# Half 0's output blocks between the steps of half 1's first modes: four blocks ahead, in other tiles

## The chip, the core and the metric

The kernel runs on one core of a Trainium2 chip. The metric is device time in microseconds (us), the median of several runs. The core has five engines that run side by side, each in its own program order: TensorE (PE, matmuls), VectorE (DVE), ScalarE (ACT), GpSimd (POOL) and SyncE (SP), which here only issues DMAs. POOL and ACT issue some DMAs too. All DMAs are carried by 16 DMA engines. SBUF has 128 partitions, and the matmuls write PSUM, in banks of 512 floats for each partition.

## The reference, cut to what matters

The program has two layers over an image of 256 x 256 x 128 floats. Layer 0 is a gated attention. Layer 1, in whose last third the change lies, is a Fourier operator block. Its 256 channels are tokens of 256 x 128 pixels, in groups of four:

```python
h0 = instance_norm(attn, norm2_w, norm2_b)
h1 = fno_layer(h0, mix_wr[0], mix_wi[0], mix_bias[0], mix_sw[0], mix_sb[0], (H, W), norm=True, act=True)
h2 = fno_layer(h1, mix_wr[1], mix_wi[1], mix_bias[1], mix_sw[1], mix_sb[1], (H, W), norm=True)
out = instance_norm(h2, mon_w, mon_b) + attn
...
def fno_layer(x, wr, wi, bias, sw, sb, out_hw, norm=False, act=False):
    skip = jnp.einsum('bihw,oi->bohw', x, sw) + sb[:, None, None]
    xf = spectral_conv(x, wr, wi, bias, out_hw)
    if norm:
        xf = instance_norm(xf)
    y = xf + skip
    return gelu(y) if act else y
```

A spectral convolution takes the few lowest Fourier modes of an image, mixes them over the four channels of a group, and turns them into an image again. The skip is a 4 x 4 mix of the channels pixel by pixel. At the end `x` (the input of the layer) is added.

## The kernel before, in words

The 256 tokens are two halves of 128, one token for each partition. An image is cut into 16 blocks of NB = 2048 pixels (two parts of HB = 1024). A large tile `blocks` holds one half's image, 16 blocks of 1 MB; `hb[b]` is block b. It is used by half 0 first and then by half 1, block after block.

Each half goes through five stages:

- `y_blocks`: the image that enters (half 0's stays in `blocks`, half 1's goes to DRAM, `yd`), with its statistics.
- `first_modes(a)` (L1624): statistics become scales on DVE; the modes are mixed (`mix_modes`: products on DVE or POOL, sums on PE); `norm` takes their energy (`x1ens`, 16 matmuls on PE) and makes rsqrt of it in some ten small steps on DVE and ACT; `synth_modes` (L728) turns the mixed modes, in four steps c0 to c3, into modes for each image row: matmuls (L764 for half 1: `g11gp`), copies by ACT and DVE into a tile `gt`, and four DMAs from the queues of POOL and ACT into DRAM (`Gd1`). Between c1 and c2 the scales of the images (`bl0`, `turn`) are made by small steps on DVE and PE.
- `first_images(a)` (L1695): for each block b, the skip (64 or 32 matmuls, L1387) and the modes' image (32 matmuls, L1372) into four PSUM banks `ups`, the gelu on ACT into `hb[b]`, which overwrites what was there. For block b - 1: transposes (`htps`), copies (`hT`), the skip's statistics (`sps`), and a Fourier step over one axis (`psA`, `yA`), written to DRAM (`Yd`). It yields twice in an iteration, once between these two groups of steps (0) and once at its end (1). Its loads of iteration b fetch block b + 1: half 1's image from `yd` in two parts (tiles of the tags wx and yt) and four DMAs of modes (gs2).
- `second_modes(0)`: the same for the second convolution, from `Yd` to `Gd2`. For half 1 it is `LastModes.run`, after the loop.
- `output(a, b)` (L2072): skip and modes' image into four banks `h2ps`, ACT scales and shifts them into `hb[b]`; a yield; then two DVE adds of `hb[b]` onto `w` (the sum of `x` and a part of the result, made earlier and kept in DRAM, `wd`) and two output DMAs of 512 KB from POOL's queue (L2085, L2086).

The order of all engines, SP's queue among them, is written out by hand in this part (`manual_schedule` with SP), so every instruction stands in its engine's queue in the order in which the Python code makes it. An instruction that waits holds all that stands behind it on its engine. Waits themselves come from the tiles: a tile of a pool and tag is one of a few buffers, and a new user of a buffer waits for the last reader of the old one. A pool that is opened after another was closed takes the same memory.

The main part (L2166 to L2229) runs half 0's stages and those of half 1, woven into each other by generators. The part around the change:

- In pool `mp1` half 0's second modes use the tiles F (4 KB for each partition), gt (8 KB), m (two of 2 KB) and f (4 KB), made in this order. Half 1's first modes `m1` run step by step with them, in tiles of the pool `xp` that stays open (tags yt, gs and xt).
- `output_0` yields after its first load, and then twice for each block: after the matmuls and ACT, and after the adds and the output DMAs. Its loads are `w_b` (1 MB) into the tag xt, of which there are three buffers, and four DMAs of modes into the tag gs.
- L2200 makes `o0`, and its first `next` loads block 0. Then `m1` runs to its end, block 0 of the output follows, and block 1 in the pool `hp1`, which is opened in the place of `mp1`; its tiles are wx (4 KB), gs2 (two of 2 KB), hT (four of 2 KB) and yA (two of 2 KB). Image 0 of half 1 uses loads that were made in `mp1` (`y2` in gt, `g2` in m).
- In the loop over `first_images(1)`, a half-step of the output follows each yield, steered by `due`: blocks 2 to 10 in iterations 0 to 8, and blocks 11 to 15 a little later. The output of block b must be finished before image b of half 1 overwrites `hb[b]`.

Of the kernel before, what the change touches and what calls it, by code (L numbers as in the profile page):

```python
# [10 lines left out]
FP = mybir.dt.float32  # L11
# [7 lines left out]
P = 128  # L19
# [681 lines left out]
def layer1(tc, I, C, ident, x1d, upool, U, Q2, groups, out):  # L701
# [6 lines left out]
    nc = tc.nc  # L708
    NT, H, W = 256, 256, 128
    L = lambda n: I["L1_conv_" + n]  # L710
    with ExitStack() as ctx:
# [86 lines left out]
        wp = gctx.enter_context(tc.tile_pool(name="wp", bufs=3))  # L798
# [363 lines left out]
        NB = 2048  # L1162
        x1v = x1d.rearrange("(a p) h w -> p a (h w)", p=P)
        xp = yctx.enter_context(tc.tile_pool(name="xp", bufs=2))
# [29 lines left out]
        wp = hctx.enter_context(tc.tile_pool(name="wp2", bufs=2))  # L1194
# [86 lines left out]
        with tc.manual_schedule(engines=COMPUTE):  # L1281
# [29 lines left out]
            m1 = sp.tile([32, NT], FP, name="m1")  # L1311
# [41 lines left out]
        ydv = yd.rearrange("(a p) x -> p a x", p=P)  # L1353
        outv = out.rearrange("(a p) h w -> p a (h w)", p=P)
        HB = NB // 2
# [36 lines left out]
        def load_modes(gs, Gd, b, tt=None):  # L1392
            for j in range(4):
                q = slice(32 * j, 32 * j + 32)
                if tt is None:
                    nc.sync.dma_start(
                        gs[q].rearrange("f n t -> f (n t)"),
                        Gd[:, j, 4 * b : 4 * b + 4, :].rearrange("f n t -> f (n t)"),
                    )
                else:  # L1400
                    nc.sync.dma_start(gs[q], Gd[:, j, 4 * b : 4 * b + 4, tt])

        def weave(main, side):

            due = 0.0
            for t in main:
                due += t
                while due > 0 and side is not None:
                    u = next(side, None)
                    if u is None:  # L1410
                        side = None
                        break
                    due -= u

        def run(stage):
            for _ in stage:
                pass
# [50 lines left out]
        halves = []  # L1468
# [10 lines left out]
        wd = dram.tile([P, 16 * NB], FP, name="wd")  # L1479
# [592 lines left out]
        def output(a, b, gs, w, psk):  # L2072

            krs, c0 = (halves[a].col[:, k : k + 1] for k in (14, 9))
            ps = [psk.tile(f"h2ps_{a}_{b}_{j}") for j in range(4)]
            skip(ps, by_turn(hb[b]), by_blocks(halves[a].bl0), False)
            image(ps, gs, bs4)
            for j in range(4):
                nc.scalar.activation(  # L2079
                    by_turn(hb[b])[:, j], rows_of(ps[j]), AF.Identity, bias=c0, scale=krs  # L2080
                )
            yield
            for s in range(2):
                px = slice(b * NB + s * HB, b * NB + (s + 1) * HB)
                nc.vector.tensor_tensor(w[s], w[s], hb[b][:, s * HB : (s + 1) * HB], ALU.add)  # L2085
                nc.gpsimd.dma_start(outv[:, a, px], w[s])  # L2086

        def output_0(psk):

            got = {}  # L2090

            def load(b):
                t = xp.tile([P, NB], FP, tag="xt", name=f"w_{b}", bufs=3)
                nc.sync.dma_start(t, wd[:, b * NB : (b + 1) * NB])
                t = [t[:, 0:HB], t[:, HB:]]
                gs = xp.tile([P, 4, P], FP, tag="gs", name=f"gs3_0_{b}", bufs=3)
                load_modes(gs, halves[0].Gd2, b)
                got[b] = t, gs

            load(0)  # L2100
            yield
            for b in range(16):
                if b not in got:
                    load(b)
                if b < 15:
                    load(b + 1)
                t, gs = got.pop(b)
                yield from output(0, b, gs, t, psk)
                yield
# [56 lines left out]
        with tc.manual_schedule(engines=COMPUTE | {ENG.SP}):  # L2166
            with tc.tile_pool(name="psy", bufs=8, space=PSUM) as psy:
                run(y_blocks(0, Banks(psy, "y"), 0, 32))
            pz = _Held(tc.tile_pool(name="pz", bufs=4, space=PSUM))
            bq, br = Banks(pz.pool, "q"), Banks(pz.pool, "r")  # L2170

            def tiles(wp):
                return Tiles(F=(wp, "F", 1), f=(wp, "f", 1), m=(wp, "m", 2))

            U1 = 24
            with tc.tile_pool(name="mp0", bufs=1) as wp:
                y1 = y_blocks(1, br, 0, U1, Sums(wp))
                weave((2.4 * t for t in first_modes(0, wp, tiles(wp), bq, [(wp, "gt", 1)])), y1)
                halves[0].sums = True
                run(y1)  # L2180
            with tc.tile_pool(name="hp0", bufs=2) as wp:
                run(first_images(0, wp, xp, bq, br))
            with tc.tile_pool(name="mp1", bufs=1) as wp:
                y1 = y_blocks(1, br, U1, 32)
                next(y1)
                m0 = second_modes(
                    0, wp, tiles(wp), bq, [(xp, "xt", 3)], [(wp, "gt", 1)] * 3 + [(xp, "xt", 3)]
                )
                weave((2.4 * next(m0) for _ in range(3)), y1)
                run(y1)  # L2190
                m1 = first_modes(
                    1, wp, Tiles(F=(xp, "yt", 2), f=(xp, "yt", 2), m=(xp, "gs", 3)), br, [(xp, "xt", 3)]
                )
                next(m1)
                for k, _ in enumerate(iter(lambda: next(m0), None)):
                    if k % 4 == 3:
                        next(m1)
                for _ in m0:
                    next(m1, None)
                o0 = output_0(bq)  # L2200
                next(o0)
                y2 = wp.tile([P, NB], FP, tag="gt", name="y2_0", bufs=1)
                nc.sync.dma_start(y2, ydv[:, 1, 0:NB])
                run(m1)
                g2 = wp.tile([P, 4, P], FP, tag="m", name="gs2_1_0", bufs=2)
                next(o0)
                load_modes(g2, halves[1].Gd1, 0)
                next(o0)
            with tc.tile_pool(name="hp1", bufs=2) as hp:
                next(o0)  # L2210
                next(o0)
                due, begun = 0.0, False
                for done in first_images(1, hp, xp, bq, br, ([y2[:, 0:HB], y2[:, HB:]], g2)):
                    if not done:
                        due += 0.9
                        begun = due > 0
                    if begun:
                        next(o0, None)
                    if done and begun:
                        due -= 1.0  # L2220
                run(o0)
            pz.release_now()
            op = ctx.enter_context(tc.tile_pool(name="op1", bufs=1))
            o1, last = Output1(op), LastModes(op)
            last.load()
            with tc.tile_pool(name="mpq3", bufs=1, space=PSUM) as psq:
                last.run(psq, o1)
            with tc.tile_pool(name="opk1", bufs=8, space=PSUM) as psk:
                o1.run(Banks(psk, "k"))  # L2229
# [118 lines left out]
def conv_preact_d2(tc, I, C, out):  # L2348
    nc = tc.nc
    NT, H, W = 256, 256, 128  # L2350
    with tc.tile_pool(name="top", bufs=1) as top, tc.tile_pool(name="x1p", bufs=1, space=DRAM) as xd:
        ident = top.tile([P, P], FP, name="ident")
        make_identity(nc, ident)
        x1d = xd.tile([NT, H, W], FP, name="x1d")
        held = _Held(tc.tile_pool(name="up", bufs=1, side="right"))
        U = held.pool.tile([P, 129, NT], FP, name="U")
        Q2 = held.pool.tile([P, NT], FP, name="Q2")
        g2 = Groups(tc, C, top)
        mv2 = held.pool.tile([P, 8, 2], FP, name="mv2")
        layer0(tc, I, C, ident, x1d, U, Q2, mv2, g2)  # L2360
        layer1(tc, I, C, ident, x1d, held, U, Q2, g2, out)
# [32 lines left out]
```

## Time and profile before

| what | us |
|---|---|
| median of three runs | 2630.17 (2627.25 to 2636.5) |
| the profiled execution | 2637.42 |
| its span, first to last instruction | 2635.7 |
| PE busy in the span | 2418.5 (92%) |
| DVE, ACT, POOL busy | 2024.6, 1422.7, 1476.0 |
| HBM read and written | 317.36 MB and 135.27 MB |

The page of the profile cuts the span into 40 slices of 66 us each; a digit is the busy share in tenths:

```profile
PE   6899999999999999999998999998979978899754
DVE  7799999999999999999997457567645645465455
ACT  0377888888888888888885122001016401565232
PEclk9999999999999999999999999999989988899855
DMA  9755565666656565665653011788877764998699
```

Layer 0 fills the first half and more. The change lies in the slices 34 to 37 (2174 to 2438 us). Slice 34 is the end of both halves' modes, slices 35 to 37 are the loop over half 1's first images with half 0's output, and the last three are half 1's last modes and its output.

The matmuls of the output's blocks 0 and 1 begin at 2241.2 and 2244.4 us, those of half 1's image 0 at 2256.8 and of image 1 at 2270.7 us; the last `psA` of the loop ends at 2439.2 us.

### The profile page before, as it was taken

The page shows a single profiled execution, that of the slowest core. Times are in us where ns is not written, and L with a number is a line of the kernel's source. Part 1 is how long each engine was busy: PE and PEld are TensorE (multiplying, and loading weights), DVE is VectorE, ACT ScalarE, POOL GpSimd, SP SyncE. Part 2 cuts the span into 40 slices and gives each one's busy share as a digit, 9 for nine tenths or more (in the row PEclk, how much of TensorE's full clock was granted, in tenths as well). Part 3 has the DMA queues.
Part 4 walks back from the last instruction along what each step waited for, and adds up shares of the span by engine and source line. Part 5 has one row for each costly group of instructions (what it writes and reads, how often), then busy time and mean ns, then how long its engine had stood idle before and what let it go on. Part 6 is the DMA issues. An engine that isn't in the chain of part 4 may idle for free. (4 is left out here: it accounts for less than half of the span.)

```text
span 2635.7 us, 88777 instructions
## 1 busy us (share of the span) xinstructions
PE 2418.5 (92%) x37590; PEld 1546.8 (59%) x37590; DVE 2024.6 (77%) x2872; ACT 1422.7 (54%) x2732; POOL 1476.0 (56%) x1043
## 2 busy tenths in 40 slices
PE   6899999999999999999998999998979978899754
PEld 5555556565556555656554567786754556455633
DVE  7799999999999999999997457567645645465455
ACT  0377888888888888888885122001016401565232
POOL 1299999999999999999995012002136411111011
PEclk9999999999999999999999999999989988899855
DMA  9755565666656565665653011788877764998699
GB/s 364 217 101 102 102 109 103 106 106 108 105 103 108 102 109 102 109 104 105 108 104 65 5 59 65 264 272 291 296 276 260 238 239 140 316 361 312 195 377 349
DMA packets 1016549, 458.49 MB, mean 174 GB/s; under 512 B 831062, under 2 KB 946729, under 8 KB 1009752
## 3 DMA queue, kind: packets, MB, share of 16 engines
q1 hardware_dynamic: 980120, 364.71, 55.0%
q0 software_dynamic: 22832, 81.54, 8.0%
q10 hardware_dynamic: 13200, 6.56, 0.9%
q8 instruction: 298, 4.88, 0.8%
q14 instruction: 99, 0.81, 0.1%
HBM read 317.36 MB, written 135.27 MB: 172 GB/s over the span
## 5 line engine op out<-in xcount | busy, mean ns | idle before, releaser
L422 POOL TENSOR_TENSOR e<-e,b1T 128x1024 f32<-128x1024 f32 x255 | 604.8, 2372 | 82.6 <-ACT e L404 82.0
L427 POOL TENSOR_TENSOR es<-e 128x512 f32<-128x512 f32 x512 | 648.9, 1289 | 0.1
L449 DVE RECIPROCAL av<-av 128x256 f32<-128x256 f32 x256 | 452.2, 1766 | 9.1
L404 ACT ACTIVATE sc<-sc,b2T 128x512 f32<-128x512 f32 x514 | 340.0, 662 | 122.4 <-PE sc L395 109.9
L404 ACT ACTIVATE e<-sc,b2T 128x512 f32<-128x512 f32 x510 | 323.4, 694 | 0.0
L420 DVE TENSOR_TENSOR e<-sc,b1T 128x1024 f32<-128x1024 f32 x257 | 312.3, 1215 | 7.1 <-ACT sc L404 3.6
L395 PE MATMUL sc<-qkT 32*128 32x256 f32 x4096 | 294.9, 401 | 1.2 <-DVE e L420 1.2
L1505 PE MATMUL yps<-xt,mpT 128*128 128x256 f32 x1024 | 249.1, 394 | 30.8 <-DMA xt<-x1d 15.0
L437 PE MATMUL av<-e,v 128*32 128x256 f32 x4096 | 268.7, 379 | 1.8 <-DVE gate L450 1.7
L395 PEld LDWEIGHTS sc<-qkT 32*128 32x128 f32 x4096 | 185.7, 184 | 113.4 <-issue 52.7
L1505 PEld LDWEIGHTS yps<-xt,mpT 128*128 128x128 f32 x1024 | 193.6, 194 | 75.7 <-DVE yt L1517 20.0
L437 PEld LDWEIGHTS av<-e,v 128*32 128x32 f32 x4096 | 130.1, 109 | 125.9 <-issue 38.5
L1521 POOL DMA_DIRECT2D yd<-yt x32 | 17.5, 546 | 324.6 <-DVE yt L1517 322.1
L367 ACT ACTIVATE qkT<-qk,qb 128x512 f32<-128x512 f32 x256 | 174.4, 681 | 3.2 <-PE qk L337 3.2
L337 PE MATMUL qk<-turned,wT_wk 128*32 128x256 f32 x2048 | 164.5, 393 | 0.4 <-DVE g_ve L35 0.4
L494 ACT ACTIVATE turned<-turned 128x256 f32<-128x256 f32 x256 | 104.4, 409 | 111.7 <-DVE x1b L462 109.4
L337 PEld LDWEIGHTS u<-adft,x 128*32 128x32 f32 x4096 | 118.5, 110 | 74.9 <-issue 74.7
L442 PE MATMUL av<-es,ones 128*32 128x256 f32 x2048 | 160.7, 379 | 1.5 <-POOL es L427 1.5
L2079 ACT ACTIVATE blocks<-h2ps,col 128x512 f32<-128x512 f32 x128 | 88.9, 779 | 130.4 <-PE h2ps L1372 130.4
L345 DVE STREAM_TRANSPOSE turned<-xk 128x1024 f32<-128x1024 f32 x128 | 158.1, 1235 | 0.4 <-DMA xk<-in_L_conv_kv_x_dram 0.4
L337 PE MATMUL qk<-turned,wn_wq 128*32 128x256 f32 x2048 | 157.9, 380 | 0.0
L2086 POOL DMA_DIRECT2D out_dram<-w x64 | 34.3, 536 | 186.6 <-DVE w L2085 186.4
(566 smaller groups left out, 4266.0 us busy)
## 6 DMA issues: line engine op xcount, KB each, us to landing
xt<-x1d SPq DMA_DIRECT2D x128, 512.0 KB, 7.2
U<-in_x_dram SPq DMA_DIRECT2D x32, 1024.0 KB, 10.3
xk<-in_x_dram SPq DMA_DIRECT2D x512, 64.0 KB, 3.0
xk<-in_L_conv_kv_x_dram SPq DMA_DIRECT2D x512, 64.0 KB, 2.6
x1d<-x1b SPq DMA_DIRECT2D x512, 64.0 KB, 2.2
out_dram<-w POOLq DMA_DIRECT2D x64, 512.0 KB, 7.9
x<-x1d SPq DMA_DIRECT2D x126, 256.0 KB, 3.4
y<-yd SPq DMA_DIRECT2D x62, 512.0 KB, 8.8
```

The lines of the kernel that those rows point to most:

```text
L337: nc.tensor.matmul(out[hd], w[:, hd], src, start=start, stop=stop)
L345: nc.vector.transpose(turned[:, a : b + 1 : b - a].rearrange("p k (b c) -> p k b c", c=32), t)
L367: nc.scalar.activation(r["qkT"], ps, AF.Identity, bias=self.qb)
L395: nc.tensor.matmul(sc[h // 2][:, h % 2, c * 256 : (c + 1) * 256], qkT[p, 256 + c * P : 256 + (c + 1) * P], qkT[p, 0:256], start=True, stop ...
L404: nc.scalar.activation(r["e"][1][:, :, c, :] if hp and s < NS - 1 else z, z, AF.Exp, bias=b2T[:, c, s : s + 1])
L420: nc.vector.tensor_tensor(e, sc.rearrange("p h x -> p (h x)"), w, ALU.mult)
L422: nc.gpsimd.tensor_tensor(e, e, w, ALU.mult)
L427: nc.gpsimd.tensor_tensor(es, e[:, :, 0, :], e[:, :, 1, :], ALU.add)
L437: nc.tensor.matmul(ps[hd, 0:256], p["v"][:, 2 * (s % 2) + c, hd], r["e"][h // 2][:, h % 2, c, :], start=(c == 0), stop=(c == 1),)
L442: nc.tensor.matmul(ps[32 * h : 32 * h + 32, 256:512], self.ones, r["es"][h // 2][:, h % 2, :], start=True, stop=True,)
L449: nc.vector.reciprocal(rd, rd)
L1505: nc.tensor.matmul(rows_of(ps[j]), mpT[:, sc, tt], by_turn(xt[:, sc])[:, j], start=(sc == 0), stop=False,)
```

## The change

`output_0` gets the pool `mp1` and a number `early`, 4. The blocks 0 to 3 no longer load into xt and gs, but into the tiles of half 0's modes: blocks 0 and 2 into F and f (a part each, with a DMA each), blocks 1 and 3 into gt, their modes into m. Block 3 doesn't load block 4 ahead. After c0 of half 1's first modes, the first yield of more than 1.2, a half-step of the output follows every yield of `m1`; what is left of the eight half-steps follows behind, all inside `mp1`. The loads of `y2` and `g2` in `mp1` go: `first_images(1)` loads its block 0 itself. In the loop, a block of the output is made in an iteration while fewer than four blocks are ahead of the images: none in iteration 0, blocks 4 to 15 in iterations 1 to 12.

```diff
-        def output_0(psk):
+        def output_0(psk, wp, early):
...
             def load(b):
-                t = xp.tile([P, NB], FP, tag="xt", name=f"w_{b}", bufs=3)
-                nc.sync.dma_start(t, wd[:, b * NB : (b + 1) * NB])
-                t = [t[:, 0:HB], t[:, HB:]]
-                gs = xp.tile([P, 4, P], FP, tag="gs", name=f"gs3_0_{b}", bufs=3)
+                px = slice(b * NB, (b + 1) * NB)
+                if b < early and b % 2 == 0:
+                    t = [wp.tile([P, HB], FP, tag=tag, name=f"w_{b}_{tag}", bufs=1) for tag in ("F", "f")]
+                    for s in range(2):
+                        nc.sync.dma_start(t[s], wd[:, b * NB + s * HB : b * NB + (s + 1) * HB])
+                else:
+                    t = (
+                        wp.tile([P, NB], FP, tag="gt", name=f"w_{b}", bufs=1) if b < early
+                        else xp.tile([P, NB], FP, tag="xt", name=f"w_{b}", bufs=3)
+                    )
+                    nc.sync.dma_start(t, wd[:, px])
+                    t = [t[:, 0:HB], t[:, HB:]]
+                gs = (
+                    wp.tile([P, 4, P], FP, tag="m", name=f"gs3_0_{b}", bufs=2) if b < early
+                    else xp.tile([P, 4, P], FP, tag="gs", name=f"gs3_0_{b}", bufs=3)
+                )
                 load_modes(gs, halves[0].Gd2, b)
                 got[b] = t, gs
...
-                if b < 15:
+                if b < 15 and b != early - 1:
                     load(b + 1)
...
-                o0 = output_0(bq)
+                early = 4
+                o0 = output_0(bq, wp, early)
                 next(o0)
-                y2 = wp.tile([P, NB], FP, tag="gt", name="y2_0", bufs=1)
-                nc.sync.dma_start(y2, ydv[:, 1, 0:NB])
-                run(m1)
-                g2 = wp.tile([P, 4, P], FP, tag="m", name="gs2_1_0", bufs=2)
-                next(o0)
-                load_modes(g2, halves[1].Gd1, 0)
-                next(o0)
+                behind = 0
+                for t in m1:
+                    behind += t > 1.2 or behind > 0
+                    if behind:
+                        next(o0)
+                for _ in range(behind, 2 * early):
+                    next(o0)
             with tc.tile_pool(name="hp1", bufs=2) as hp:
-                next(o0)
-                next(o0)
-                due, begun = 0.0, False
-                for done in first_images(1, hp, xp, bq, br, ([y2[:, 0:HB], y2[:, HB:]], g2)):
-                    if not done:
-                        due += 0.9
-                        begun = due > 0
-                    if begun:
+                ahead, done = early, 0
+                for part in first_images(1, hp, xp, bq, br):
+                    if not part:
+                        due = ahead < 16 and ahead < done + 4
+                    if due:
                         next(o0, None)
-                    if done and begun:
-                        due -= 1.0
+                    if part:
+                        ahead, done = ahead + due, done + 1
                 run(o0)
```

## The prediction

> **What bounds the kernel now.** I read the table of stretches first, cut where the change works: the last steps of half 1's first modes with blocks 0 and 1 of half 0's output and the first image of half 1 (2214 to 2263 us), then the loop of `first_images(1)` in four pieces.
>
> ```profile
> core 0: us, PE busy (x) PEld busy (x) DVE busy (x) ACT busy (x) POOL busy (x), PEclk, DMA share, GB/s
> 2214.00:2263.00 49.00, 37.17 (x766) 28.34 (x766) 13.38 (x31) 11.07 (x19) 8.15 (x12) 0.65 0.68 220
> 2263.00:2283.00 20.00, 16.66 (x283) 7.56 (x284) 6.02 (x8) 12.50 (x18) 1.07 (x2) 0.91 0.95 319
> 2283.00:2368.00 85.00, 79.05 (x1732) 44.96 (x1728) 52.77 (x73) 52.94 (x80) 14.67 (x24) 1.00 1.02 358
> 2368.00:2393.00 25.00, 21.48 (x372) 12.74 (x368) 11.41 (x17) 10.68 (x17) 2.60 (x4) 0.86 0.88 300
> 2393.00:2440.00 47.00, 44.16 (x864) 23.61 (x864) 31.90 (x45) 25.56 (x40) 8.12 (x13) 1.00 0.92 321
> ```
>
> In the first stretch TensorE runs at 0.65 of its clock and still stands for 12 us; the DMAs move 220 GB/s. In the loop TensorE is 93% busy and the DMAs are full (358 GB/s). So two blocks' work is to leave a full stretch for a loose one. What holds the loose one shows in the chain of waits there, and in what SP's queue waited for:
>
> ```profile
> 2219.32 3.59 PE x1ens L1608 x16
> 2228.31 1.29 DVE g11gt L772 x2
> 2238.84 4.71 DMA Gd<-g11gt
> 2243.85 0.34 SPq L2094
> 2244.24 8.30 DMA gs<-Gd
> 2252.59 3.35 PE h2ps L1372 x30
> ```
>
> ```profile
> SPq L2094 <- DMA Gd<-g20gt: 49.4, 1, 49.4
> SPq L2094 <- DMA Gd<-g11gt: 24.8, 1, 24.8
> ```
>
> The load of block 1 (L2094) sits 24.8 us at the head of SP's queue for a tile of the tag xt, until half 1's modes have been written from it; TensorE then waits for block 1's modes until 2252.6. But up to 2241 the chain is another: small dependent steps of half 1's modes, PE to DVE to ACT and back. The timeline and the list of DMA issues (size, median us to landing) give the prices:
>
> ```profile
> 2222.93 0.16 DVE L35 TENSOR_SCALAR rq_ve<-x1ens 128x1 f32<-128x1 f32 x1 [2.90 <-PE x1ens L1608]
> 2225.11 3.28 PE L764 MATMUL g11gp<-x1Z,k_esyn 32*64 32x128 f32 x116 [1.57 <-DVE col L1618]
> 2243.55 2.79 ACT L2079 ACTIVATE blocks<-h2ps,col 128x512 f32<-128x512 f32 x4 [1.52 <-PE h2ps L1372]
> 2246.37 2.36 DVE L2085 TENSOR_TENSOR w<-w,blocks 128x1024 f32<-128x1024 f32 x2 [4.01 <-ACT blocks L2079]
> 2247.89 0.55 POOL L2086 DMA_DIRECT2D out_dram<-w  x1 [2.54 <-DVE w L2085]
> gs<-Gd SPq DMA_DIRECT2D x384, 64.0 KB, 5.3
> out_dram<-w POOLq DMA_DIRECT2D x64, 512.0 KB, 7.9
> ```
>
> **What the Trainium skill says.** "DMA: Bandwidth & Descriptors", section on the anatomy of one DMA: the DMA engines don't wait for semaphores, the issuing sequencer does before it dispatches. The 24.8 us of L2094 agree, and they make SP's order part of the cost. The same section says that a DMA's semaphore comes only when the last byte is confirmed in the target; here an output write (512 KB) took 7.22 us from issue to landing at 2247.9 and 5.08 us at 2260.3, so a tile that is written out and then reused costs about 6 us after its last instruction. "TensorE: Matmul & The Clock Gate", Part 1: the clock is halved after an idle window and restored by sustained work. The trace agrees: 0.50 from 2214.2 to 2227.8, 2231.2 to 2241.5 and 2251.7 to 2262.0 us, and 128 matmuls of L764 take 3.72 us there against 2.09 us in half 0 at the full clock.
>
> **The change part by part.** All in the profiled execution's own time (2637.42 us, span 2635.7), which lies 7.25 us above the median of the runs.
>
> Where things go. `m1` yields more than 1.2 first after its synthesis step c0, so the first half-step of the output (matmuls, ACT) comes behind c0, then one after each of its five other yields, then two more: blocks 0 to 3 are all issued before `hp1` opens. Before, blocks 0 and 1 were. In the loop, `due` starts in iteration 1 with block 4 and ends in iteration 12 with block 15: 12 outputs in iterations 1 to 12, where there were 14 in iterations 0 to 9 and 11 to 14.
>
> *The moved steps join half 1's dependent chain.* (1) Block 0's modes are issued on SP by 2218.3 as before (they wait for Gd2); with 5 us they land at 2223.3, so PE, which reaches them at about 2221, waits; its 32 image matmuls at half clock (2.2; 1.2 warm, 2.7 at 2381.6) end at 2225.5. (2) `x1ens` comes behind them. Block 0's ACT evacuation 2.79 -> 2228.3, and its two DVE adds 2.36 -> 2230.7 stand ahead of the rsqrt steps on DVE; those take 2.1 (2222.93 to 2225.05) -> 2232.8. (3) Only then has c1 its last bank: 3.28 -> 2236.1 (before 2228.4), copies 1.29 -> 2237.4, block 1's adds 2.36 -> 2239.8, ahead of the bl multiply on DVE; from there to c2 3.0 as before -> 2242.8. (4) c2 3.7 -> 2246.5, block 2's matmuls 3.2 (2.07 + 1.10, the loop's steady L1387 and L1372) -> 2249.7, c3 3.0 (2.1 to 4.4) -> 2252.7, block 3's 3.2 -> 2255.9. Its modes: SP's load(3) waits for block 1's output, 2239.8 + 0.3 + 6 = 2246.1, then w (0.35), four issues (2.0) and 5 = 2253.5, just in time. On this path c3 ends 11 us later than before (2241.3).
>
> *A wait that the change adds.* `hp1` opens on the memory that mp1 leaves: its wx (4 KB) lies on F, its two gs2 and half of its hT on gt, by the order and the sizes in which both pools make their tiles. In before those were long free, and `y2_0` and `g2` were fetched ahead. Now F and gt hold blocks 2 and 3, so image 0's modes (gs2, at the head of SP's queue, all other loads behind it) wait for block 3's output: 2255.9 + 2.79 + 2.36 + 0.3 + 6 = 2267.4, issues 2.0, landing 5 -> 2274.4, matmuls 1.3 -> 2275.7, against 2262.5 before: **+13.2 us**. y2_0 waits for block 2's output only (2262) and is ready first.
>
> *What comes back.* Iteration 0 has no output between: before, image 1 started 8.2 us after 2262.5 (block 2 in between); now 1.3 (table load) and 0.7 to 0.9 for a bank, 2.9 at most: **-5.3**. Iteration 1: load(4) is issued only at its use, behind y2_5, which waits for image 1's matmuls; its modes land some 12 us after image 1 begins and PE wants them after 7.5. The iteration takes about 15.8 where it took 12.3 (2270.7 to 2283.0): **+3.5**. From there one output fewer. An iteration with one takes 10.46 us (2283.0 to 2293.5), without 8.5 (the last, 2425.9 to 2434.4): **-2.0**. DMA crowding: from 2283.0 to 2425.9 the 13 iterations took 142.9, of which 12 x 10.46 + 8.5 = 134.0 are explained; 8.9 are crowding (gs<-Gd 10.1 us at 2371). Eleven full iterations in a row now ask for 3.75 MB each (w 1, y 1, out 1, modes and Yd 0.75), 10.1 us at the 370 GB/s seen at best (2340 to 2360): still crowded, but the last three are free; I take **-1** (0 to -6).
>
> Sum: 13.2 - 5.3 + 3.5 - 2.0 - 1 = +8.4 us: 2645.8 for the profiled execution, **2638.5** as a median (2630.17 + 8.4).
>
> Edits at nothing: splitting w_0 and w_2 into two DMAs (SP then idle, +0.35 each); fewer xt and gs tiles; leaving out the fetch of y2_0 and g2 is inside the +13.2. SP waits 10 us in load(2), with nothing but these loads behind it. POOL writes c1's Gd behind block 0's output; needed after 2267, so hidden. The last modes after the loop still start from the last Yd write (2439.86) and pay the same.
>
> Bounds: the shortest prices (landing 4.3, output 5, matmuls at the full clock) put image 0's end at 2268.1: +5.6 - 5.3 + 2 - 2 - 6 = -5.7. The longest (output 8, landing 5.5, half clock) put it at 2284: +21.5 - 5.3 + 4 - 2 = +18.
>
> **Rivals.** *No wait for the memory* (faster): if the first tiles of hp1 don't lie on F and gt, or the loads find them free, image 0 follows block 3 directly: 2255.9 + 3 = 2258.9, -3.6 - 5.3 + 3.5 - 2, and with the crowding gone (-5) -12.4: 2618. For it: the page shows 220 GB/s and 12 us of idle PE in the stretch, and the wait of 24.8 us is surely gone. Against: the sizes above. It decides from an image 0 ended by about 2263. *Evens out*: prices nearer the short end, 2630 (-6 to +6). For it: every term is a few us. Against: outputs land late where the DMAs are busy (median 7.9). *Slower by more*: each of the two turns through memory (out, load of modes) at the loaded prices of 2359 (9.4 out) or of POOL's Gd at 2243.9 (8.9), and the clock at half throughout: 2648. All of the change happens as the code says; that it wouldn't is no case I find.
>
> **Numbers.** Forecast, +6 to +16 (2636 to 2646): 0.42; slower by more 0.10; evens out 0.25; faster 0.23. A measurement of this kernel tells about 0.3% (7.9 us) from no change; 0.04 of the forecast's case lies inside that. So slower 0.38 + 0.10 = 0.48, same 0.25 + 0.04 = 0.29, faster 0.23. The range is 2616 to 2650: it takes in the faster case's centre and the slowest one's.
>
> **What would show it.** Right: c2 (L764) begins 8 to 11 us later than 2232.5; gs<-Gd of image 0 waits on out_dram; PE idle 10 us or more between block 3's matmuls and image 0's; image 1 close behind image 0; a stall of 3 to 5 us at block 4's modes; three short iterations at the end. Wrong if image 0's matmuls end before 2266, or if the loop from image 2 to the last psA takes less than 148 us (156.2 before).

## The result and the profile after

The changed kernel took 2638.5 us in the median of eight runs (2634.75 to 2647.16), the kernel before 2633.07 us in as many runs beside them (2627.25 to 2648.52). The ratio is 1.0026, with a 95% interval of 1.001 to 1.0043. A second set of runs of the changed kernel gave 1.0021 (1.0005 to 1.0037). So the change costs some 5 to 7 us: the interval lies above 1, but the size is just under the 0.3% that the prediction counts as measurable.

The two first profiles say the opposite: 2634.75 us for the profiled execution after (span 2633.0), 2637.42 us before. What differs is the stretch that the change touches, so I measure it from a landmark that both kernels have, c0, the first `g11gp` matmul of half 1, and use three profiles of the kernel before and two of the one after (the sections below say where the others are from). All times are us from c0.

| | c3 ends | block 3 of the output, matmuls end | image 0 ends | image 1 starts | image 2 starts | image 15 starts | last psA ends |
|---|---|---|---|---|---|---|---|
| before, first profile | 26.3 | in the loop | 47.6 | 55.7 | 68.0 | 210.9 | 224.2 |
| before, second | 23.6 | in the loop | 45.3 | 53.0 | 65.3 | 205.6 | 218.8 |
| before, third | 23.8 | in the loop | 45.7 | 53.8 | 66.0 | 205.7 | 218.9 |
| after, first profile | 30.8 | 39.7 | 56.7 | 57.4 | 77.1 | 212.2 | 224.9 |
| after, second | 31.4 | 40.0 | 57.1 | 58.0 | 79.4 | 215.2 | 227.9 |

The first profile of before holds one loop iteration of 15.1 us that the other two don't have; against these two the change adds 6 to 9 us. Over all five profiles the stretch averages 220.6 us before and 226.4 after, 5.8 more, which fits the medians. What follows the last psA takes 194.5 to 197.8 us in every profile of this study.

The chain of waits of the kernel after (start, us, what) shows where the stretch now hangs. Before, it hung on c3's `Gd` write and the load of block 1's modes.

```profile
2230.74 10.36 DMA out_dram<-w x2
2241.23 7.68 DMA w<-wd
...
2256.95 3.19 DMA out_dram<-w
2260.51 0.34 SPq L1707
2260.91 4.61 DMA y<-yd
...
2275.83 6.98 DMA gs<-Gd
```

Three turns through memory stand in it, in which something waits until a tile has been written out or loaded. Block 1's output must land before block 3's loads may start in its tile; block 3's output must land before `y2_0` may be fetched into `hp1`; and block 4's modes are fetched only when they are needed. The waits of SP's queue in the stretch (in total, times, longest) name the first two (L2103 loads the output's `w`, L1707 the images' `y2`); the 24.8 us of L2094 for `g11gt` are gone:

```profile
SPq L1707 <- DMA out_dram<-w: 16.3, 1, 16.3
SPq L2103 <- DMA out_dram<-w: 10.6, 1, 10.6
```

Block 2's loads wait too, 9.3 us for block 0's output, but that wait is not on the chain.

PE's timeline has the price of each in its brackets: 4.34, 12.24 and 4.06 us of idle PE.

```profile
2249.16 2.69 PE L1372 MATMUL h2ps<-k_bsyn,gs 32*128 32x128 f32 x32 [4.34 <-DMA gs<-Gd]
2264.10 1.17 PE L1387 MATMUL ups<-y,bl 32*32 32x256 f32 x32 [12.24 <-DMA y<-yd]
2269.59 4.18 PE L1387 MATMUL ups<-y,bl 32*32 32x256 f32 x64 [0.78 <-ACT blocks L1750]
2282.86 2.69 PE L1372 MATMUL h2ps<-k_bsyn,gs 32*128 32x128 f32 x32 [4.06 <-DMA gs<-Gd]
```

The third line, image 1's skip, has little idle time but a price too: its 64 matmuls take 4.18 us where they take 1.50 in the loop at full clock. PE's clock is at 0.50 from 2249.8 to 2273.7 us, but that is the smaller part: image 0's 64 skip matmuls, at the same clock, took 1.17 us for each half, 2.34 in all. The rest is a wait that the merged line hides: PE begins each of the four banks 0.05 us after ACT has finished image 0's gelu from that bank. The kernel before (second profile) waits for ACT at this place too, at full clock:

```profile
2268.94 3.30 PE L1387 MATMUL ups<-y,bl 32*32 32x256 f32 x64 [0.85 <-ACT blocks L2079]
```

So half the clock costs 0.9 us here against the kernel before.

The table of stretches is cut here at c0, image 2, image 15 and the last psA, first of the kernel after, then of the second profile of the kernel before (columns as in the prediction's table; the last three are PE's clock, the DMAs' share and GB/s):

```profile
2212.00:2289.00 77.00, 49.61 (x1110) 32.50 (x1110) 20.43 (x39) 25.76 (x40) 10.35 (x16) 0.76 0.77 258
2289.00:2424.00 135.00, 125.37 (x2684) 70.01 (x2680) 84.72 (x117) 80.70 (x122) 22.69 (x37) 0.99 0.99 346
2424.00:2437.00 13.00, 13.00 (x212) 6.65 (x208) 8.46 (x14) 5.01 (x8) 1.51 (x2) 1.00 0.72 228
```

```profile
2216.00:2281.00 65.00, 50.34 (x1046) 32.53 (x1046) 18.60 (x36) 22.74 (x35) 9.19 (x14) 0.77 0.79 258
2281.00:2422.00 141.00, 129.99 (x2780) 71.54 (x2777) 84.75 (x117) 83.99 (x128) 22.73 (x37) 1.00 1.01 347
2422.00:2435.00 13.00, 12.81 (x199) 6.59 (x175) 10.82 (x17) 4.82 (x9) 2.57 (x4) 1.00 0.88 304
```

Read the last column, GB/s, with the length. Over the whole stretch both move the same: 19.9 + 46.7 + 3.0 = 69.5 MB after, 16.8 + 48.9 + 4.0 = 69.6 MB before. In the loop both move 346 to 347 GB/s with the DMAs full: 46.7 MB in 135 us, 48.9 MB in 141 us. If bytes set the loop's length, what counts is how far the DMAs fall short of 347 GB/s at the two ends. Before image 2 the kernel after takes 77 us for bytes that need 19.9 / 0.347 = 57.3 us and loses 19.7; the kernel before loses 65 - 48.3 = 16.7. In the last 13 us, where the kernel after has no output left to write and PE is 100% busy, it loses 13 - 8.5 = 4.5, the kernel before 13 - 11.4 = 1.6. Together 3.0 + 2.9 = 6 us.

With equal bytes and an equal rate in the loop, though, this sum must come out at the difference, whatever sets the loop's length. Single iterations tell more. Here are those of images 2 and 3 in the kernel after:

```profile
2289.22:2299.65 10.43, 9.78 (x221) 5.49 (x217) 6.64 (x10) 6.63 (x10) 1.83 (x3) 1.00 0.83 295
2299.65:2310.08 10.43, 9.78 (x222) 5.49 (x218) 6.64 (x10) 6.63 (x10) 1.84 (x3) 1.00 1.03 380
```

They take the same 10.43 us at 295 and at 380 GB/s, with PE busy for 9.78 us and idle for 0.65 behind a step of DVE. Eight of the loop's eleven iterations with an output take this long, and the two without one 7.92 us. At these lengths the loop from image 2 to image 15 would last 130.6 of the 135.1 us measured; the other 4.5 us stand in three iterations of 10.7, 11.7 and 13.4 us. For the kernel before, the shortest lengths seen at each place of its loop (eight of 10.47 us, then 7.97, 10.54 and three of 10.93; its profiles and that of e7_w1, whose loop has the same order) make 135.1 us, where its second and third profile took 140.3 and 139.6. So the excess is alike, 4.5 and 5.2 us in both kernels' two profiles (7.8 in the first of before), and the loop is shorter after because it holds one output less and because its last outputs take 10.43 us and not 10.93. Full DMAs alone don't show that bytes set the loop's time: in the kernel after, most of its iterations have the length of PE's work and one step of DVE.

### The profile page after: what moved, and what is told of

It reads as the page before. It is cut to its first block, busy times and chain, and to the rows that moved or that the text cites. A ratio compares the mean times of both kernels' runs of the same rounds, so it can differ in the third digit from the quotient of the medians.

```text
span 2633.0 us, 88739 instructions
## 1 busy us (share of the span) xinstructions
PE 2407.2 (91%) x37590; PEld 1541.2 (59%) x37590; DVE 2024.1 (77%) x2872; ACT 1421.0 (54%) x2732; POOL 1474.4 (56%) x1043
## 5 line engine op out<-in xcount | busy, mean ns | idle before, releaser
L1505 PE MATMUL yps<-xt,mpT 128*128 128x256 f32 x1024 | 246.8, 391 | 31.1 <-DVE yt L1517 13.8
L337 PE MATMUL u<-adft,x 128*32 128x129 f32 x4096 | 137.0, 273 | 0.0
```

The lines of the kernel that those rows point to most:

```text
L337: nc.tensor.matmul(out[hd], w[:, hd], src, start=start, stop=stop)
L1505: nc.tensor.matmul(rows_of(ps[j]), mpT[:, sc, tt], by_turn(xt[:, sc])[:, j], start=(sc == 0), stop=False,)
```

## The experiments

The theory (A) was that of the prediction: the change pays for the turns through memory that it adds, image 0's loads behind block 3's output and block 4's loads at their use, and without them it would be faster. The rivals: (B) the loop is bound by DMA, so that what is gained ahead of it is given back in it; (C) what costs is that the output's steps stand between the dependent steps of half 1's modes.

Each "stretch" below runs from c0 to the last psA, in one profile. Profiles of one kernel differ by 3 to 5 us there, so a stretch is read together with the ratio of the times.

**The changed kernel again**, as the partner of the next three; no edit.

> The changed kernel once more, unedited. The stretch from c0's first matmul (L764, g11gp) to the loop's last psA was 224.2 us before and 224.9 after in the two profiles at hand, while the medians say +5.4 us. If the stretch is as long here as in the first profile (224 to 226), nearly all of the difference of the medians lies elsewhere or in the spread of the runs; if the loop's crowding varies between executions, it will be 226 to 232 here, and the ratio of the times stays at 1.001 to 1.004.

Ratio 1.0021 (1.0005 to 1.0037), stretch 227.9. The second line of "after" in the table is this profile: idle PE of 12.32 us ahead of image 0 and of 4.79 us at block 4's modes.

**Other places for image 0's tiles.** The prediction derived the wait from bytes: wx on F, gs2 on gt. Here the tiles that are loaded first are made in a second pool behind the first, so that wx lies on m and gs2 on f, and only hT and yA on F and gt.

```diff
-        def first_images(a, wp, yp, psk, pst, first=None):
+        def first_images(a, wp, yp, psk, pst, first=None, lp=None):
+            lp = lp or wp
...
-                        pool, tag, bufs = (wp, "wx", 1) if k % 3 == 0 else (yp, "yt", 2)
+                        pool, tag, bufs = (lp, "wx", 1) if k % 3 == 0 else (yp, "yt", 2)
...
-                gss[b] = wp.tile([P, 4, P], FP, tag="gs2", name=f"gs2_{a}_{b}")
+                gss[b] = lp.tile([P, 4, P], FP, tag="gs2", name=f"gs2_{a}_{b}")
...
-            with tc.tile_pool(name="hp1", bufs=2) as hp:
+            with tc.tile_pool(name="hp1", bufs=2) as hp, tc.tile_pool(name="hp1l", bufs=2) as lp:
...
-                for part in first_images(1, hp, xp, bq, br):
+                for part in first_images(1, hp, xp, bq, br, lp=lp):
```

> Image 0's tiles (wx, gs2) lie on m and f, hT and yA on F and gt. Theory A (the wait of image 0's loads for block 3's output costs time): the loads go out at about 2254 instead of 2260.5, image 0's matmuls end 5 to 7 us earlier behind c0 (56.6 us in the changed kernel), and the stretch from c0 to the last psA is 4 to 7 us shorter than 224.9, ratio to before about 0.999. Rival B (the loop is bound by its DMAs): image 0 is earlier, but the stretch is the same within 2 us. Rival C (what costs is the lengthening of c0 to c3, 26.3 to 30.7 us): no gain beyond 1 us.

A miss: ratio 1.003 (1.0017 to 1.0043), stretch 227.0. From its table of waits and its chain:

```profile
SPq L1709 <- DMA out_dram<-w: 18.6, 1, 18.6
```

```profile
2265.30 4.41 DMA out_dram<-w
2270.08 0.34 SPq L1709
2270.47 4.78 DMA y<-yd
```

`y2_0` is still issued only behind block 3's last output write (2265.30 + 4.41 = 2269.71, issue 2270.08), although its tile is that of block 3's modes, which the matmuls had read by 2260, and block 2's outputs from f had landed by 2267.0. In the kernel after it is the same: y2_0's tile lies on F, whose last output, issued at 2246.46, landed some 6 us later, and y2_0 is issued at 2260.51, after block 3's. If the tiles lie as their sizes and order say, the wait is thus not one of overlapping bytes: the first tile of a pool opened in the place of another waited, in both placements, for the last work on the old pool.

**Block 4 loaded ahead**, in block 3's turn, as every other block is.

```diff
-                if b < 15 and b != early - 1:
+                if b < 15:
```

> Block 3 loads block 4 ahead, as every other block does for its next. Theory A: the stall of PE at block 4's modes (2278.8 to 2282.9, then 2.6 us at half clock) goes, iteration 1 takes 13 to 14 us instead of 19.6 (image 1 to image 2), the stretch is 5 to 6 us shorter, ratio about 0.999. Rival B: the 1 MB and the modes land earlier, but the loop is as long within 2 us.

Ratio 0.9986 (0.9966 to 1.0007), beside 1.0021 for the changed kernel in the same set (medians 2635.77 and 2640.61 us); stretch 223.7. The stall is gone and the step from image 1 to image 2 takes 13.8 us where it took 19.6 and 21.4. From PE's timeline:

```profile
2288.94 2.10 PE L1387 MATMUL h2ps<-blocks,bl 32*32 32x512 f32 x32
2290.97 1.17 PE L1372 MATMUL h2ps<-k_bsyn,gs 32*128 32x128 f32 x32
```

The block's modes matmuls follow its skip with no idle time between. The loop up to image 15 takes 139.1 us, though, where it took 135.1 and 135.8: 6 to 8 us are gained ahead of it and 3 to 4 given back in it, at 336 GB/s instead of 346.

**Both edits together.**

> Both edits. Theory A: the gains add up, the stretch is 10 to 12 us shorter than 224.9 (213 to 215), ratio to before 0.996 to 0.998. Rival B: the stretch stays above 220, since the twelve full iterations then only crowd the DMAs more.

Ratio 1.0016 (1.0 to 1.0032), stretch 222.5, image 0's end at 57.9. The other placement adds nothing here either. The ratio is 0.3% above that of e2_load4, the stretch 1 us below; so much for how finely edits of this size can be told apart. The edit of e2_load4 is in here whole, and yet this ratio shows no gain over the changed kernel that is clear of the intervals.

**Image 0 loaded ahead, outside `hp1`.** e2_load4, and the first block of half 1's image and its modes go into tiles of the pool `xp`, which is open all along; so both added waits are gone.

```diff
-                for _ in range(behind, 2 * early):
-                    next(o0)
+                y2 = xp.tile([P, NB], FP, tag="xt", name="y2_0", bufs=3)
+                nc.sync.dma_start(y2, ydv[:, 1, 0:NB])
+                next(o0)
+                g2 = xp.tile([P, 4, P], FP, tag="gs", name="gs2_1_0", bufs=3)
+                load_modes(g2, halves[1].Gd1, 0)
+                next(o0)
...
-                for part in first_images(1, hp, xp, bq, br):
+                for part in first_images(1, hp, xp, bq, br, ([y2[:, 0:HB], y2[:, HB:]], g2)):
```

> Image 0's loads go into xt and gs of the pool that stays open (y2 behind block 2's half-steps, the modes behind block 3's matmuls), and block 4 is loaded ahead. Theory A (revised: hp1 as a whole waits for the last output from mp1, which moving its tiles did not change): image 0 ends 45 to 49 us behind c0 instead of 56.7, iteration 1 is short, and the stretch from c0 to the last psA is 8 to 11 us shorter than in the changed kernel (224.9 and 227.9): 215 to 218, ratio to before 0.996 to 0.998. Rival B (the loop's DMAs take it back): image 0 is early, the stretch is 221 or longer.

Ratio 0.9991 (0.998 to 1.0001), stretch 215.1: 10 us less than the kernel after, 4 less than before. Image 0's end moves by only 2 us, to 54.7, for another chain comes up behind the one removed:

```profile
2249.58 6.22 DMA Gd<-g11gt
2255.93 6.09 DMA gs<-Gd
2262.06 1.97 PE ups L1372 x6
```

POOL's last write of c3's modes takes 6.2 us to land, image 0's load of them 6.1; PE stands for 7.7 us. That is the chain which bounded the kernel before at block 1, now met at image 0.

**Three blocks ahead in place of four.**

```diff
-                early = 4
+                early = 3
```

> Three blocks ahead instead of four, nothing else. Theory A: hp1 opens on block 2's output, which lands at 2254.2 instead of 2260.1, so image 0 ends about 6 us earlier behind c0 (50 to 52); the loop has one output more (+2.5), so the stretch is 3 to 4 us shorter than in the changed kernel (222 to 224). Rival B: the loop's DMAs have 2.25 MB more to carry in it, 6 us at 370 GB/s, and the stretch is as long or longer (225 to 230).

Ratio 1.0013 (1.0 to 1.0025), stretch 227.8. The turn for block 3 is gone and image 0 ends at 52.1, 5 us earlier than with four blocks. But one more output is made in the loop, iteration 0 takes 10.2 us instead of 0.8, so that image 2 starts only 2 to 4 us earlier (75.0). The loop to image 15 then takes 140.0 us instead of 135.1 and 135.8, and the end is where it was. That is the outcome which rival B foretold; what lengthened the loop isn't shown.

**Four blocks behind the modes, not between their steps**, in the same tiles.

```diff
-                behind = 0
-                for t in m1:
-                    behind += t > 1.2 or behind > 0
-                    if behind:
-                        next(o0)
-                for _ in range(behind, 2 * early):
+                run(m1)
+                for _ in range(2 * early):
                     next(o0)
```

> The eight half-steps all follow behind the end of half 1's first modes; tiles and loop as in the changed kernel. c0 to c3 returns to 26 us. Theory A: the turns through F, f and gt then come one after the other behind c3: image 0 ends at about 68 us behind c0 (56.7 in the changed kernel), the stretch takes 233 to 237, ratio 1.005 to 1.007. Rival C (the interleaving itself costs more than it saves, through c0 to c3): the stretch is at most 225.

Ratio 1.0085 (1.0063 to 1.0107), stretch 244.1. c3 ends at 24.1, some 7 us earlier, as C has it; but the turns through memory now come one after the other with nothing beside them. PE's timeline, at block 2 and at image 0:

```profile
2267.23 2.67 PE L1372 MATMUL h2ps<-k_bsyn,gs 32*128 32x128 f32 x32 [8.04 <-DMA gs<-Gd]
...
2288.34 1.17 PE L1387 MATMUL ups<-y,bl 32*32 32x256 f32 x32 [12.80 <-DMA y<-yd]
```

Image 0 ends at 69.6. So C falls for these tiles: standing between the steps of the modes is worth 16 to 19 us against standing behind them, more than it costs their chain. For tiles without these turns C wasn't tested.

**The kernel before, with block 1's loads freed.** Its 24.8 us of waiting at L2094 come from the tag xt. Here block 1 alone loads into F, f and m; all else is the kernel before.

```diff
             def load(b):
-                t = xp.tile([P, NB], FP, tag="xt", name=f"w_{b}", bufs=3)
-                nc.sync.dma_start(t, wd[:, b * NB : (b + 1) * NB])
-                t = [t[:, 0:HB], t[:, HB:]]
-                gs = xp.tile([P, 4, P], FP, tag="gs", name=f"gs3_0_{b}", bufs=3)
+                if b == 1:
+                    t = [wp.tile([P, HB], FP, tag=tag, name=f"w_{b}_{tag}", bufs=1) for tag in ("F", "f")]
+                    for s in range(2):
+                        nc.sync.dma_start(t[s], wd[:, b * NB + s * HB : b * NB + (s + 1) * HB])
+                    gs = wp.tile([P, 4, P], FP, tag="m", name=f"gs3_0_{b}", bufs=2)
+                else:
...
```

> The kernel before, with one edit: block 1 loads into F and f and m, so the wait of 24.8 us at the head of SP's queue goes. Block 1's matmuls then follow block 0's at about 2249 instead of 2256; image 0 still needs its modes, whose last writes land at 2254, so it ends 2 to 4 us earlier behind c0 than 47.6, and the stretch is 2 to 4 us shorter than 224.2, ratio 0.998 to 0.9995. If the loop is bound by its DMAs (rival B), the stretch is within 1 us of before.

Ratio 1.0005 (0.9991 to 1.0018), stretch 218.5. PE no longer stops at block 1, and image 0 ends at 40.3 instead of 45.3 to 47.6. Nothing of it reaches the end. The table of stretches, cut at the same marks:

```profile
2215.00:2276.00 61.00, 48.05 (x1046) 29.95 (x1035) 18.41 (x36) 22.80 (x35) 9.20 (x14) 0.83 0.78 256
2276.00:2420.00 144.00, 132.72 (x2748) 73.23 (x2744) 84.29 (x116) 83.76 (x127) 22.77 (x37) 0.98 1.00 347
```

The loop begins 4 us earlier, but with 61 x 0.256 = 15.6 MB moved instead of 16.8; it has 50.0 MB to move at the same 347 GB/s where it had 48.9, and takes 144 us instead of 141. So freeing the wait of 24.8 us gained nothing that the times show. Why is open: the bytes fit, but this one profile also holds an iteration of 16.0 us, much like the one of 15.1 us in the first profile of before.

**Repeats**: the kernel before twice more, for its profile, and e4_ahead once more.

> The kernel before once more, unedited, for a second profile of its loop and for what the measurement makes of no change. The loop's crowding varies: the stretch from c0 to the last psA was 224.2 us in the first profile, with one iteration of 15.5 us. The medians of the edits (0.9991 for the stretch of 215.1, 1.0005 for the one of 218.5) put it at 217 to 220 here; if it is 223 to 226 again, the medians hold something outside the stretch. Ratio 0.999 to 1.001.

> A third profile of the kernel before: the stretch lies between 216 and 226 us, and the part up to image 1 (55.7 us behind c0) varies less than the loop behind it (168.5).

> The version with image 0's and block 4's loads ahead once more: the stretch is 214 to 219 us, ratio to before 0.998 to 1.000, and so below the changed kernel by 0.2 to 0.4%.

The kernel before against itself: 0.9993 (0.9979 to 1.0006), stretch 218.8; the third, in one run, 2630.69 us and 218.9. e4_ahead again: 0.9991 (0.9979 to 1.0002), stretch 220.3 with image 0's end at 55.2 and a loop of 139.2 us instead of 134.5. Against the kernel before, e4_ahead is 0.1% faster in both sets, with both intervals just reaching 1; against the changed kernel it is some 0.3% faster (0.9991 / 1.0021, from different sets).

**c3's writes of modes from SP.** On e4_ahead, whose image 0 waits for POOL's last write of them.

```diff
-                            queues=(nc.gpsimd, nc.scalar))
+                            queues=(nc.sync if a and c == 3 else nc.gpsimd, nc.scalar))
```

> As the version with the loads ahead, and of c3's four writes the two of POOL's queue go from SP's. There the last write landed at 2255.8 (POOL, 6.2 us after issue), and image 0's modes could only be loaded then. Theory A: the write lands 2 to 3 us earlier, image 0 ends at 51 to 53 us behind c0 instead of 54.7, the stretch is 1 to 3 us shorter, ratio 0.997 to 0.999. Rival B: the loop takes it back, the stretch is as long.

A miss: ratio 0.9995 (0.9983 to 1.0008), image 0's end at 58.0, three us later than in e4_ahead, stretch 221.3. SP waits 4.6 us for c3's copies with its loads queued behind, and PE idles 7.6 us for y2_0 and then 6.0 us for its modes. No version that was run is shown to beat the kernel before.

What this leaves of the three: e4_ahead, in two sets, lies below the changed kernel by about what the change costs, and the intervals don't overlap (up to 1.0001 and 1.0002 against 1.0005 and more). So A is right in that the change pays for the two waits that e4_ahead takes away; how much each costs isn't told apart, and that without them it would be faster than before isn't shown. B foretold the outcomes of e5_early3 and e7_w1, but not that of e4_ahead (221 us or longer, against 215.1 and 220.3), and its mechanism isn't shown: the excess of the loop over its shortest iterations was 3.9 and 8.6 us in two profiles of e4_ahead itself, and 7.6 us in e6_behind, which starts its loop last of all.

## Why the prediction was right, and where its steps were off

The predicted 2638.5 us was measured, and the mechanism was as put down: image 0's loads behind block 3's output, 12.24 us of idle PE there (10 or more foreseen), image 1 close behind image 0, a stall of 4.06 us at block 4's modes (3 to 5 foreseen), three short iterations at the end. The agreement to the microsecond is luck twice over. The forecast was 2630.17 + 8.4; the kernel before then came out at 2633.07, and the change at +5.4 by the medians (+6.8 by the ratio), at the lower edge of the +6 to +16 forecast. And several terms were off and cancelled. Measured as after (two profiles) less before (second and third), the terms are:

| term | predicted | measured |
|---|---|---|
| image 0's end | +13.2 | +11 to +12 |
| iteration 0 | -5.3 | -7 |
| iteration 1 | +3.5 | +7 to +9 |
| image 2 to the end, with crowding | -3 | -4 to -6 |
| sum | +8.4 | +6 to +9 |

- **The moved steps join half 1's chain.** Mis-sized. Block 0's modes were expected to hold PE; they had landed. Its matmuls ended 6.0 us after c0, not 10.5, c2 began at 21.3, not 27.8, and c3 ended at 30.8, not 37.7. So c2 came 4 to 5.5 us later than before, not the 8 to 11 that the prediction named as its sign. Also PE, busy with block 0, was at full clock from 2215.7 us, and 116 of c1's matmuls took 1.98 us instead of 3.28.
- **Block 3's own modes.** "Just in time" failed: block 1's outputs took 9.1 and 9.8 us to land, where I had put 6. load(3) was issued at 2241.2 and PE idled 4.34 us. Block 3's matmuls ended at 39.7, against 40.9 predicted: one error gave back what the other took.
- **The wait for `hp1`.** It was there, at about its size, for a wrong reason in its form. `y2_0` was expected ahead of the modes, after block 2's output, at 2262; it waited for block 3's output itself. e1_placed speaks against the overlap of bytes on which I built it. Block 3's outputs landed in 2.9 and 3.2 us instead of 6, which made the term smaller.
- **Iteration 1.** The stall had its size, the step not. I had left out that PE does much of this iteration at half clock. Against the second profile of before, the skip took 4.18 instead of 3.30 us, block 4's 32 modes matmuls 2.69 instead of 1.17, and the skip's statistics 2.01 instead of 1.23: 3.2 us, which with the stall of 4.06 make up the 7.3 us that the iteration is longer. e2_load4 removes the late load and with it 6 to 8 us of this step.
- **The loop.** Iterations without an output took 7.9 us, not 8.5, so one output less is worth 2.5 us and not 2.0. The other 2 to 3 us need no crowding: the last outputs of the kernel before take 10.93 us each in all its profiles, which I had counted as crowding, and after they take 10.43. The limit set for "wrong", 148 us from image 2 to the last psA, lies between the two profiles, 147.9 and 148.6, so by that sign alone the first would count against the forecast.
- **The rivals.** "No wait for the memory" would have given 2618 us. e4_ahead takes both waits away and stays at 2629.6 (2631.0 for the kernel before in its set), as image 0 then waits for its own modes. So that rival had not only the wrong condition but also too large a gain.

What stays open: why the chain of e1_placed, e2_load4 and e4_ahead has a pause of 2.4 to 2.7 us inside c3's matmuls that the profile puts down to nothing it shows, how the loop comes to move 336 GB/s in one profile and 350 in another, and what lengthens the few long iterations. None of these was tried, and no run took bytes or PE's work out of the loop, so how much of its time either sets isn't measured.

## What to carry to other kernels

Before you call a loop bound by its DMAs, look at single iterations: this one kept the DMAs 99% busy, and still most of its iterations took the same time at 295 and at 380 GB/s. A long wait in a queue is not a gain to be had: freeing one of 24.8 us brought nothing that the times show. Tiles that are written out and then loaded again chain two landings and a load, so put such turns between other work. The first tiles of the next phase can go into a pool that is already open, which took away the wait here, though what that alone is worth wasn't measured. When terms of a few us with both signs make up the forecast, one profile of each kernel isn't enough to compare: here the first pair had the wrong sign.

## What the runs showed of the hardware

- The landing of one and the same 512 KB output write varied more than its list of medians (7.8 us) lets one expect: 2.9 and 3.2 us with the DMAs otherwise idle (issued at 2255.8 and 2257.0), 9.1 and 9.8 us beside loads and the modes' writes (2230.7 and 2231.3). Both stood on the chain within 30 us of each other.
- In this program the first tile of a newly opened pool waited for the last DMA out of the pool before it, in whichever place it was put (issued 0.4 us after that landing in both placements).
- Across orders that differ in the start of the loop by 32 us, from 61 us after c0 to 93, the full part of the loop moved 336 to 351 GB/s, and the whole stretch 69.3 to 69.7 MB.
- Two iterations of the same work took 10.43 us each, while the DMAs were 0.83 busy at 295 GB/s in one and 1.03 busy at 380 GB/s in the other.
- 64 skip matmuls took 1.50 us at full clock and 2.34 at half clock where their banks were free, and 3.30 and 4.18 where PE waited for ACT bank by bank. The two delays add up.
